# A bidirectional Mamba layer and a ConvLSTM on one core: dt and C copied to DRAM four times over before they are spread over the partitions

## The chip, the cores and the metric

The kernel runs on 1 core of a Trainium2 chip. The metric is the device time of one execution in microseconds (us). Before the change it is 7981.35 us, the median of 3 runs (7974.65 to 7982.71).

## The reference

The input is an image of 64 channels by 256 times by 128 frequencies, in float32. The first layer runs a bidirectional Mamba block along time and then another along frequency, each with a residual. The second layer is a windowed, bidirectional ConvLSTM. Everything that matters here is in the Mamba block:

```python
xdbl = jnp.einsum('nld,ed->nle', x, p['x_proj_w'])
dt, Bm, Cm = jnp.split(xdbl, [DT_RANK, DT_RANK + D_STATE], axis=-1)
dt = jax.nn.softplus(jnp.einsum('nlr,dr->nld', dt, p['dt_proj_w']) + p['dt_proj_b'])
A = -jnp.exp(p['A_log'])

def step(h, inp):
    dt_t, B_t, C_t, x_t = inp
    dA = jnp.exp(dt_t[:, :, None] * A)
    h = dA * h + dt_t[:, :, None] * B_t[:, None, :] * x_t[:, :, None]
    return (h, jnp.einsum('nds,ns->nd', h, C_t))
```

There are 128 inner channels (D_INNER) with 16 states each, so 2048 recurrences run side by side, forwards and backwards.

## The kernel before

**Tiles.** Stage 0 runs along time (sequences of 256 tokens), stage 1 along frequency (128 tokens). Each stage goes through 64 chunks of 512 tokens (NTOK), in two directions d. The 128 partitions of a scan hold 4 states (j, NJ) by 32 channels (DB); a row of a scan holds two states (g) by 512 tokens. A chunk and direction therefore has 8 scan steps: two groups of states (q) by 4 blocks of channels (b, NB). A chunk has 16 steps, and step S of the whole stage is step S mod 16 of its chunk.

**One step.** PE makes dt·B·x for the step (`inputs`, tile bx, L570) from dtxT and the diagonal matrices D (L460 on DVE). ACT makes exp(dt·A) (`decays`, tile dA, L590) from rep. DVE scans (`recur`, L598). POOL multiplies by C (`outputs`, L604). PE folds four steps into y (`add_up`, L613). DVE multiplies y by the gate (`gate`, tile yz, L629) at steps 2 and 10. A dA tile has four buffers, bx two, h seven.

**The spreads.** The decays need dt of 32 channels on 128 partitions, four times over, and POOL needs each of four rows of C on 32 partitions. Both go through DRAM. `dt_away` writes dt to the DRAM tile there in four transfers of 64 KB (L392); `project_bc` makes B and C with PE (L415), copies them out of PSUM with ACT (L424) and writes C to the DRAM tile away in four transfers of 8 KB per direction (L433). `spread_dt` (L475, tile rep, 3 buffers) and `spread_c` (L469, tile C, 3 buffers) read 512 KB each back, with the repetition in the source's access pattern. There are four of each per chunk. The source of `spread_c` has the shape 4 (j) by 32 (repeated) by 1024, that of `spread_dt` 4 (repeated) by 32 by 1024.

**Other transfers.** `normalise` (POOL, tile xn) writes the normalised input into the padded tile unp, by four transfers within SBUF (L308); `project_x` (L327, L328 on PE, copy L346 on ACT) and `project_z` read unp. In stage 0 `load` brings the input u (L282).

**Order.** Every engine works through its instructions in the order in which they are written, and all these transfers are issued by SyncE (SP). `Stage.run` goes through the steps S and writes, for each: the scan of S, outputs of S - 1, `add_up` when S mod 4 is 1, inputs and decays of S + 2, and then what the list HEAD has for that step. HEAD gives, for the chunk that begins at slot 16, the slot of each of its preparations: slot 6, for example, is step 6 of the chunk before, slot 17 is step 1 of its own, and half slots come after the closing of the chunk before. Negative slots lie one chunk earlier still. `first` prepares the first chunk of each stage, in an order of its own; SECOND is what it leaves to the loop.

The lines of HEAD that bear on the change are

```python
(-13, "load"),
(8, "project_bc", 0, 1),
(8, "dt_away", 0),
(8.5, "dt_away", 1),
(9.5, "spread_dt", 0, 0),
(10.5, "spread_c", 0, 0),
```

Of the kernel before, what the change touches and what calls it, by code (L numbers as in the profile page):

```python
# [29 lines left out]
F32 = mybir.dt.float32  # L30
# [6 lines left out]
P = 128  # L37
# [3 lines left out]
NS = 16  # L41
NBC = 2 * NS
NB = 4
NJ = 4
DB = P // NB
NU = 4
W = 64
RANK = 4
NTOK = 512
# [20 lines left out]


HEAD = (
    (-13, "load"),
    (-7.5, "squares"),
    (-6, "means"),
    (-6, "rms"),
# [4 lines left out]
    (6, "silus"),  # L81
    (6, "step_sizes"),
    (7, "softplus"),
    (8, "project_bc", 0, 1),
    (8, "dt_away", 0),
    (8.5, "dt_away", 1),
    (8.5, "times_x", 0),
    (9.5, "spread_dt", 0, 0),
    (10, "turn", 0),
    (10.5, "spread_c", 0, 0),  # L90
    (11, "diagonal", 0, 0, 0),
    (12, "spread_dt", 0, 1),
    (12.5, "times_x", 1),
    (13, "diagonal", 0, 0, 1),
    (13.5, "spread_c", 0, 1),
    (15, "diagonal", 0, 1, 0),
    (17, "diagonal", 0, 1, 1),
    (17, "spread_dt", 1, 0),
# [6 lines left out]
    (23, "diagonal", 1, 1, 0),  # L105
    (25, "diagonal", 1, 1, 1),
)
SECOND = tuple(x for x in HEAD if x[0] >= 12)


class Mamba:
# [3 lines left out]
    def __init__(self, ctx, tc, cols, room, d):  # L115
        nc = tc.nc
        self.nc, self.tc, self.d, self.cols = nc, tc, d, cols
        cp = ctx.enter_context(tc.tile_pool(name="m_const", bufs=1))
        self.ident = cp.tile([P, P], F32, name="ident")
        self.mask = cp.tile([P, W], F32, name="mask")  # L120
        self.fold = cp.tile([P, DB], F32, name="fold")
        self.ones = cp.tile([P, P], F32, name="ones")
        self.eps = cp.tile([P, 1], F32, name="eps")
        self.Wbc = cp.tile([P, 4, NBC], F32, name="wbc")
        self.cb, self.dtb, self.dp = (cols[:, 4 * n : 4 * n + 4] for n in range(3))
        self.A = cols[:, 12 : 12 + 4 * NS].rearrange("p (i n) -> p i n", i=4)
        self.G1, self.G2, self.Wz, self.Wdt, self.W2, self.W3 = ([] for _ in range(6))
        for i in range(4):
            for n, t, rows, width in (
                ("g1", self.G1, P, P),  # L130
                ("g2", self.G2, P, P),
                ("wdt", self.Wdt, P, P),
                ("w2", self.W2, P, C),
            ):
                t.append(cp.tile([rows, width], F32, name=f"{n}{i}", tag=f"{n}{i}"))
        for i in range(2):
            self.Wz.append(cp.tile([P, P], F32, name=f"wz{i}", tag=f"wz{i}"))
            self.W3.append(cp.tile([P, 2, C], F32, name=f"w3{i}", tag=f"w3{i}"))
        b = cp.tile([P, 2], F32, name="lin_b")
        self.b = b  # L140

        room = room.rearrange("p t f -> p (t f)")
        at = 0

        def take(rows, *shape):
            nonlocal at
            n = int(np.prod(shape))
            t = room[0:rows, at : at + n]
            at += n
            return t  # L150

        self.win = take(C, 4, 2 * P + 1).rearrange("p (i n) -> p i n", i=4)
        self.cw = take(C, 4, 4, P).rearrange("p (i k n) -> p i k n", i=4, k=4)
        self.xdt = take(RANK, 8, P).rearrange("p (i n) -> p i n", i=8)
        self.ow = take(C, 4, P).rearrange("p (i n) -> p i n", i=4)
        self.lin = take(C, 4, C).rearrange("p (i n) -> p i n", i=4)


        nc.vector.memset(self.ones, 0.0)
        for h in range(2):  # L160
            own = slice(h * C, (h + 1) * C)
            nc.vector.memset(self.ones[own, own], 1.0 / C)
        nc.vector.memset(self.eps, RMS_EPS)
        for w3 in self.W3:
            nc.vector.memset(w3, 0.0)
        make_identity(nc, self.ident)
# [57 lines left out]
class Stage:  # L224
# [162 lines left out]

    def dt_away(self, ch, d):

        there = self.dram.tile([DB, NB, NTOK], F32, name="there", tag="there")  # L390
        for b in range(NB):
            self.nc.sync.dma_start(out=there[:, b], in_=self.at["dt", ch, d][DB * b : DB * (b + 1)])  # L392
        self.at["there", ch, d] = there

    def in_turns(self, ap, order):

        return ap.rearrange(order, i=2, u=NU)

# [11 lines left out]
    def project_bc(self, ch, *ds):  # L410

        nc = self.nc
        pb = self.mm("pb")
        for d in ds:
            nc.tensor.matmul(  # L415
                pb[NBC * d : NBC * (d + 1)],
                lhsT=self.m.Wbc[:, 2 * self.stage + d],
                rhs=self.at["xs", ch, d],
                start=True,
                stop=True,  # L420
            )
        bc = self.wk.tile([2 * NBC, NTOK], F32, name="bc", tag="bc")
        rows = slice(NBC * ds[0], NBC * (ds[-1] + 1))
        nc.scalar.copy(  # L424
            self.in_turns(bc[rows], "p (u i c) -> p i u c"), self.in_turns(pb[rows], "p (i u c) -> p i u c")
        )
        for d in ds:
            away = self.dram.tile([NS // 2, 2, 2, NTOK // 2], F32, name="away", tag="away")
            for g in range(2):
                first = NBC * d + NS + NS // 2 * g  # L430
                c = self.in_turns(bc[first : first + NS // 2], "p (u i c) -> p i u c")
                for i in range(2):
                    nc.sync.dma_start(out=away[:, i, g].rearrange("a (u c) -> a u c", u=NU), in_=c[:, i])  # L433
            self.at["bc", d], self.at["away", ch, d] = bc[NBC * d : NBC * d + NS], away

    def turn(self, ch, d):
# [28 lines left out]

    def spread_c(self, ch, d, q):
        t = self.wk.tile([P, 2 * NTOK], F32, name="C", tag="C", bufs=3)
        away = self.at["away", ch, d].rearrange("(j q) i g t -> q j (i g t)", q=2)[q]
        self.nc.sync.dma_start(out=t, in_=away.unsqueeze(1).to_broadcast([NJ, DB, 2 * NTOK]))  # L469
        self.at["C", ch, d, q] = t  # L470

    def spread_dt(self, ch, d, h):
        t = self.wk.tile([P, 2, NTOK], F32, name="rep", tag="rep", bufs=NREP)
        there = self.at["there", ch, d]
        self.nc.sync.dma_start(  # L475
            out=t, in_=there[:, 2 * h : 2 * h + 2].unsqueeze(0).to_broadcast([NJ, DB, 2, NTOK])
        )
        self.at["rep", ch, d, h] = t

    def head(self, ch):  # L480
# [731 lines left out]
def _layouts(a):  # L1212

    L0 = {k[8:]: v for k, v in a.items() if k.startswith("L0_conv_")}
    L1 = {k[8:]: v for k, v in a.items() if k.startswith("L1_conv_")}

    def taps(w):

        return w.reshape(256, C, 4, 2, 5).transpose(3, 1, 4, 2, 0).reshape(P, 5, 4, 256)

    def gates(f, b):

        return np.concatenate([f.reshape(2, P), b.reshape(2, P)]).T

    return {
        "x": a["x"][0].transpose(0, 2, 1),
        "cols": np.concatenate(
            [
                L0["conv_b"].T,
                L0["dt_proj_b"].T,  # L1230
                L0["Dp"].T,

                L0["A_log"].reshape(4, NB, DB, NJ, 4).transpose(3, 2, 0, 1, 4).reshape(P, 4 * NS),
                gates(L1["b_ih_f"], L1["b_ih_b"]),
                gates(L1["b_hh_f"], L1["b_hh_b"]),
                np.tile(np.stack([L1["gln_g"], L1["gln_b"], L1["b_proj"]], 1), (2, 1)),
                np.broadcast_to(L1["prelu_a"].reshape(1, 1), (P, 1)),
            ],
            1,
        ),  # L1240

        "in_proj": np.concatenate([L0["in_proj_w"].transpose(2, 0, 1), L0["norm_w"].T[:, :, None]], 2),
        "conv_w": L0["conv_w"][:, :, 0, :].transpose(0, 2, 1),
        "dt_proj": np.concatenate(
            [L0["x_proj_w"][:, :RANK].transpose(1, 0, 2), L0["dt_proj_w"].transpose(2, 0, 1)], 1
        ),
        "x_proj_bc": np.concatenate(
            [L0["x_proj_w"][:, RANK : RANK + NS], L0["x_proj_w"][:, RANK + NS :: 2], L0["x_proj_w"][:, RANK + NS + 1 :: 2]], 1
        ).transpose(2, 0, 1),
        "out_proj": L0["out_proj_w"].transpose(1, 0, 2),  # L1250
        "lin_w": np.concatenate([L0[n + "_w"].reshape(2, C, C) for n in ("tlin", "flin")]).transpose(1, 0, 2),
        "lin_b": np.stack([L0["tlin_b"], L0["flin_b"]], 1),
        "W_ih_f": taps(L1["W_ih_f"]),
        "W_ih_b": taps(L1["W_ih_b"]),
        "W_hh_f": L1["W_hh_f"][:, :, 0].T,
        "W_hh_b": L1["W_hh_b"][:, :, 0].T,
        "W_proj": L1["W_proj"].reshape(P, C, 4, 2).transpose(0, 2, 3, 1).reshape(P, 4, P),
    }
# [18 lines left out]
```

## Time and profile before

| | |
|---|---|
| median of 3 runs | 7981.35 us |
| the profiled execution | 7979.07 us |
| its span | 7977.3 us |
| PE busy | 5895.4 us (74%) |
| DVE busy | 6357.9 us (80%) |
| ACT busy | 4741.7 us (59%) |
| POOL busy | 5563.0 us (70%) |
| DMA, hardware queue | 674.33 MB, 25.2% of 16 engines |
| mean granted TensorE clock | 0.895 |

Busy time is the time in which an engine carries out instructions, and the share is of the span. The last 690 us or so belong to the ConvLSTM, the rest to the two Mamba stages. Groups of instructions are named by their line; "x" counts them, and the number after the bar gives their busy time, the mean of one in ns, and the idle time of the engine just before them with what ended it. "SPq" is SyncE's queue, on which the row of a transfer is its issue, not its flight.

### The profile page before, as it was taken

How to read it: one execution, taken by the hardware profiler on the slowest of the kernel's cores; microseconds unless marked ns; L12 is line 12 of the kernel's file. 1: busy time of each engine (PE TensorE's matmuls, PEld its weight loads, DVE VectorE, ACT ScalarE, POOL GpSimd, SP SyncE). 2: the span in 40 equal slices, each digit the busy share in tenths (PEclk: the TensorE clock that was granted, in tenths of full speed). 3: DMA queues.
4: the chain of work that ended last, by engine and by line, in shares of the span. 5: the costliest groups of instructions: out<-in, count | busy, mean ns of one | idle time of the engine just before them, and what ended most of it. 6: DMA issues, size and time to landing. Idle time of an engine off the chain costs nothing. (4 is left out here: it accounts for less than half of the span.)

```text
span 7977.3 us, 325404 instructions
## 1 busy us (share of the span) xinstructions
PE 5895.4 (74%) x149512; PEld 3497.4 (44%) x149512; DVE 6357.9 (80%) x4166; ACT 4741.7 (59%) x8600; POOL 5563.0 (70%) x2898
## 2 busy tenths in 40 slices
PE   6776776767676776776777777777776777777999
PEld 3343433434343433333444444434443434335887
DVE  7887878788787878786788787878787878786887
ACT  6665666666565666665666565656565656664333
POOL 5776777677777777776777777777777767675554
PEclk8888988889898989888889888889898888888999
DMA  2222222222222222222222322222222222221000
GB/s 89 98 93 96 94 97 92 95 95 96 95 94 97 94 97 93 97 92 79 97 95 98 96 95 94 92 91 92 93 91 94 92 93 91 94 89 72 13 15 17
DMA packets 302064, 695.14 MB, mean 87 GB/s; under 512 B 72852, under 2 KB 129812, under 8 KB 300696
## 3 DMA queue, kind: packets, MB, share of 16 engines
q1 hardware_dynamic: 300696, 674.33, 25.2%
q8 instruction: 1173, 19.22, 1.1%
q14 instruction: 195, 1.60, 0.1%
HBM read 557.25 MB, written 83.89 MB: 80 GB/s over the span
## 5 line engine op out<-in xcount | busy, mean ns | idle before, releaser
L604 POOL TENSOR_TENSOR h<-h,C 128x1024 f32<-128x1024 f32 x2048 | 4821.6, 2372 | 1782.9 <-DVE h L598 1282.2
L598 DVE TENSOR_TENSOR_SCAN h<-dA,bx 128x1024 f32<-128x1024 f32 x2048 | 4615.6, 2276 | 1403.8 <-ACT dA L590 1063.9
L590 ACT ACTIVATE dA<-rep,cols 128x510 f32<-128x510 f32 (+1 forms) x4096 | 2648.1, 711 | 874.6 <-DMA rep<-there 874.6
L570 PE MATMUL bx<-D,dtxT 64*32 64x128 f32 x131072 | 2418.5, 281 | 900.3 <-DVE h L598 880.8
L570 PEld LDWEIGHTS bx<-D,dtxT 64*32 64x32 f32 x131072 | 1901.4, 108 | 2044.1 <-issue 881.7
L460 DVE TENSOR_TENSOR D<-mask,bt 128x1024 f32<-128x1024 f32 x1026 | 1226.7, 1196 | 10.8 <-PE bt L447 10.8
L613 PE MATMUL y<-h,fold 128*32 128x512 f32 x8192 | 1212.2, 660 | 5.0 <-POOL h L604 5.0
L327 PE MATMUL px<-unp,g 128*128 128x512 f32 x504 | 399.8, 886 | 1067.3 <-DMA unp<-xn 1067.3
L346 ACT ACTIVATE xs<-px,cols 128x512 f32<-128x512 f32 x252 | 173.4, 688 | 1191.6 <-PE px L328 1191.5
L327 PEld LDWEIGHTS px<-unp,g 128*128 128x128 f32 x504 | 100.3, 249 | 1123.3 <-DMA unp<-xn 903.9
L613 PEld LDWEIGHTS y<-h,fold 128*32 128x32 f32 x8192 | 257.6, 116 | 596.9 <-issue 585.5
L403 POOL TENSOR_TENSOR dtx<-dt,xs 128x512 f32<-128x512 f32 x256 | 327.7, 1280 | 80.4 <-ACT dt L379 80.4
L328 PE MATMUL px<-unp,g 128*128 128x512 f32 x504 | 365.9, 819 | 0.0
L449 ACT COPY dtxT<-pt 128x512 f32<-128x512 f32 x256 | 149.8, 585 | 312.4 <-PE pt L445 312.3
L369 PE MATMUL pv<-xs,wdt 128*128 128x512 f32 x512 | 276.9, 666 | 49.0 <-ACT xs L363 47.5
L328 PEld LDWEIGHTS px<-unp,g 128*128 128x128 f32 x504 | 132.6, 263 | 190.5 <-issue 190.5
L1162 POOL TENSOR_TENSOR y<-v,X 128x512 f32<-128x512 f32 x32 | 40.6, 1269 | 231.2 <-DVE v L1160 231.2
L587 ACT COPY dA<-zeros 128x4 f32<-128x4 f32 (+1 forms) x1024 | 197.5, 193 | 2.2 <-DVE h L598 0.8
L629 DVE TENSOR_TENSOR yz<-y,zs 128x512 f32<-128x512 f32 x256 | 171.4, 670 | 13.5 <-PE y L613 10.8
L625 ACT ACTIVATE y<-xs,cols 128x512 f32<-128x512 f32 x256 | 175.6, 686 | 7.0 <-DVE yz L629 7.0
L671 PE MATMUL po<-yz,w 128*64 128x256 f32 x1024 | 170.9, 399 | 0.0
L445 PE MATMUL pt<-ident,dtx 128*128 128x128 f32 x1024 | 168.6, 287 | 0.8 <-POOL dtx L403 0.8
(189 smaller groups left out, 5122.5 us busy)
## 6 DMA issues: line engine op xcount, KB each, us to landing
rep<-there SPq DMA_DIRECT2D x512, 512.0 KB
C<-away SPq DMA_DIRECT2D x512, 512.0 KB
there<-dt SPq DMA_DIRECT2D x1024, 64.0 KB
unp<-xn SPq DMA_DIRECT2D x504, 64.0 KB
away<-bc SPq DMA_DIRECT2D x1024, 8.0 KB
u<-in_x SPq DMA_DIRECT2D x128, 64.0 KB
out<-y SPq DMA_DIRECT2D x32, 256.0 KB
w<-in_W_ih_f SPq DMA_DIRECT2D x10, 512.0 KB
```

The lines of the kernel that those rows point to most:

```text
L327: nc.tensor.matmul(self.seqs(px), lhsT=m.G1[i], rhs=self.unp[:, :, first : first + L], start=True, stop=False)
L328: nc.tensor.matmul(self.seqs(px), lhsT=m.G2[i], rhs=self.unp[:, :, second : second + L], start=False, stop=True)
L369: self.nc.tensor.matmul(pv, lhsT=self.m.Wdt[i], rhs=self.at["xs", ch, d], start=True, stop=True)
L403: self.nc.gpsimd.tensor_mul(self.in_turns(dtx, own), self.in_turns(self.at["dt", ch, d], natural), self.in_turns(self.at["xs", ch, d], nat ...
L460: self.nc.vector.tensor_mul(D, self.m.mask.unsqueeze(1).unsqueeze(1).to_broadcast([P, n, 2, W]), b.unsqueeze(3).to_broadcast([P, n, 2, W]),)
L570: self.nc.tensor.matmul(bx[DB * j : DB * (j + 1), i, :, u], lhsT=dtxT[rows, u, DB * b : DB * (b + 1)], rhs=D[rows, u, j], start=True, stop ...
L587: nc.scalar.copy(dA[:, :, :, :, first : first + 1], self.zeros)
L590: nc.scalar.activation(dA[:, :, g, :, live], rep[:, :, :, live], AF.Exp, scale=m.A[:, k, n : n + 1])
L598: self.nc.vector.tensor_tensor_scan(h[:, step], dA[:, step], bx[:, step], 0.0, ALU.mult, ALU.add)
L604: self.nc.gpsimd.tensor_mul(h, h, self.at["C", ch, d, q])
L613: nc.tensor.matmul(y[DB * b : DB * (b + 1)].rearrange("p (i t) -> p i t", i=2), lhsT=self.m.fold, rhs=hs[b][:, g], start=False, stop=q == ...
L625: self.nc.scalar.mul(self.y, self.at["xs", ch, d], self.m.dp[:, i : i + 1])
```

## The change

`dt_away` writes each block of dt four times, once for each j, so that there has four copies; `spread_dt` then reads 128 rows, each once. `project_bc` makes C twice in PSUM: the rows for B in the order of before (they are copied to bc with the tokens in turns, and the C rows beside them there are padding), and C's 16 rows, in another order, in the upper 64 partitions, which a second ACT copy takes over in token order. away has four copies of each row of C (NR), and `spread_c` reads 16 rows (4 states by 4 copies), each repeated 8 times. The weights for this projection double in size, to 128 KB, with zero padding. In HEAD `dt_away` of direction 0 comes ahead of `project_bc`, `dt_away` of direction 1 moves from slot 8.5 to slot 14, the first `spread_c` from 10.5 to 10, and `load` from -13 to -12.

```diff
+NR = 4
...
-    (-13, "load"),
+    (-12, "load"),
...
+    (8, "dt_away", 0),
     (8, "project_bc", 0, 1),
-    (8, "dt_away", 0),
-    (8.5, "dt_away", 1),
...
-    (10.5, "spread_c", 0, 0),
+    (10, "spread_c", 0, 0),
...
+    (14, "dt_away", 1),
...
-SECOND = tuple(x for x in HEAD if x[0] >= 12)
+SECOND = tuple(x for x in HEAD if x[0] >= 12 and x[1] != "dt_away")
...
-        there = self.dram.tile([DB, NB, NTOK], F32, name="there", tag="there")
+        there = self.dram.tile([NJ, DB, NB, NTOK], F32, name="there", tag="there")
         for b in range(NB):
-            self.nc.sync.dma_start(out=there[:, b], in_=self.at["dt", ch, d][DB * b : DB * (b + 1)])
+            dt = self.at["dt", ch, d][DB * b : DB * (b + 1)]
+            self.nc.sync.dma_start(
+                out=there[:, :, b].rearrange("j d t -> d j t"), in_=dt.unsqueeze(1).to_broadcast([DB, NJ, NTOK])
+            )
...
+        for n in range(2):
+            for d in ds:
+                first = 2 * NBC * n + NBC * d
+                nc.tensor.matmul(
+                    pb[first : first + NBC],
+                    lhsT=self.m.Wbc[:, 2 * self.stage + d, n],
...
+        rows = slice(2 * NBC + first, 2 * NBC + last)
+        nc.scalar.copy(bc[rows], pb[rows])
         for d in ds:
-            away = self.dram.tile([NS // 2, 2, 2, NTOK // 2], F32, name="away", tag="away")
+            away = self.dram.tile([NS // 2, NR, 2, 2, NTOK // 2], F32, name="away", tag="away")
             for g in range(2):
-                first = NBC * d + NS + NS // 2 * g
-                c = self.in_turns(bc[first : first + NS // 2], "p (u i c) -> p i u c")
+                first = 2 * NBC + NBC * d + NS // 2 * g
+                c = bc[first : first + NS // 2].rearrange("p (i t) -> p i t", i=2)
                 for i in range(2):
-                    nc.sync.dma_start(out=away[:, i, g].rearrange("a (u c) -> a u c", u=NU), in_=c[:, i])
+                    nc.sync.dma_start(
+                        out=away[:, :, i, g], in_=c[:, i].unsqueeze(1).to_broadcast([NS // 2, NR, NTOK // 2])
+                    )
...
-        away = self.at["away", ch, d].rearrange("(j q) i g t -> q j (i g t)", q=2)[q]
-        self.nc.sync.dma_start(out=t, in_=away.unsqueeze(1).to_broadcast([NJ, DB, 2 * NTOK]))
+        away = self.at["away", ch, d][NJ * q : NJ * (q + 1)].rearrange("j r i g t -> (j r) (i g t)")
+        self.nc.sync.dma_start(out=t, in_=away.unsqueeze(1).to_broadcast([NJ * NR, DB // NR, 2 * NTOK]))
...
-        there = self.at["there", ch, d]
-        self.nc.sync.dma_start(
-            out=t, in_=there[:, 2 * h : 2 * h + 2].unsqueeze(0).to_broadcast([NJ, DB, 2, NTOK])
-        )
+        there = self.at["there", ch, d].rearrange("j d b t -> (j d) b t")
+        self.nc.sync.dma_start(out=t, in_=there[:, 2 * h : 2 * h + 2])
```

More of the change, by code (lines that the diff above doesn't have):

```diff
@@ L123, in __init__ @@
         self.eps = cp.tile([P, 1], F32, name="eps")
-        self.Wbc = cp.tile([P, 4, NBC], F32, name="wbc")
+        self.Wbc = cp.tile([P, 4, 2, NBC], F32, name="wbc")
         self.cb, self.dtb, self.dp = (cols[:, 4 * n : 4 * n + 4] for n in range(3))
@@ L413, in project_bc @@
         pb = self.mm("pb")
[L414 to L420, printed above, removed]
-            )
-        bc = self.wk.tile([2 * NBC, NTOK], F32, name="bc", tag="bc")
-        rows = slice(NBC * ds[0], NBC * (ds[-1] + 1))
+        for n in range(2):
[4 more added lines that the diff above has]
+                    lhsT=self.m.Wbc[:, 2 * self.stage + d, n],
+                    rhs=self.at["xs", ch, d],
+                    start=True,
+                    stop=True,
+                )
+        bc = self.wk.tile([P, NTOK], F32, name="bc", tag="bc")
+        first, last = NBC * ds[0], NBC * (ds[-1] + 1)
+        rows = slice(first, last)
         nc.scalar.copy(
@@ L426, in project_bc @@
         )
+        rows = slice(2 * NBC + first, 2 * NBC + last)
+        nc.scalar.copy(bc[rows], pb[rows])
         for d in ds:
-            away = self.dram.tile([NS // 2, 2, 2, NTOK // 2], F32, name="away", tag="away")
+            away = self.dram.tile([NS // 2, NR, 2, 2, NTOK // 2], F32, name="away", tag="away")
             for g in range(2):
-                first = NBC * d + NS + NS // 2 * g
-                c = self.in_turns(bc[first : first + NS // 2], "p (u i c) -> p i u c")
+                first = 2 * NBC + NBC * d + NS // 2 * g
+                c = bc[first : first + NS // 2].rearrange("p (i t) -> p i t", i=2)
                 for i in range(2):
-                    nc.sync.dma_start(out=away[:, i, g].rearrange("a (u c) -> a u c", u=NU), in_=c[:, i])
+                    nc.sync.dma_start(
+                        out=away[:, :, i, g], in_=c[:, i].unsqueeze(1).to_broadcast([NS // 2, NR, NTOK // 2])
+                    )
             self.at["bc", d], self.at["away", ch, d] = bc[NBC * d : NBC * d + NS], away
@@ L473, in spread_dt @@
         t = self.wk.tile([P, 2, NTOK], F32, name="rep", tag="rep", bufs=NREP)
-        there = self.at["there", ch, d]
-        self.nc.sync.dma_start(
-            out=t, in_=there[:, 2 * h : 2 * h + 2].unsqueeze(0).to_broadcast([NJ, DB, 2, NTOK])
-        )
+        there = self.at["there", ch, d].rearrange("j d b t -> (j d) b t")
+        self.nc.sync.dma_start(out=t, in_=there[:, 2 * h : 2 * h + 2])
         self.at["rep", ch, d, h] = t
@@ L1246, in _layouts @@
         ),
-        "x_proj_bc": np.concatenate(
-            [L0["x_proj_w"][:, RANK : RANK + NS], L0["x_proj_w"][:, RANK + NS :: 2], L0["x_proj_w"][:, RANK + NS + 1 :: 2]], 1
-        ).transpose(2, 0, 1),
+        "x_proj_bc": np.pad(
+            np.stack(
+                [
+                    L0["x_proj_w"][:, RANK : RANK + NS],
+                    L0["x_proj_w"][:, RANK + NS :].reshape(4, NJ, 2, 2, P).transpose(0, 3, 2, 1, 4).reshape(4, NS, P),
+                ],
+                1,
+            ),
+            ((0, 0), (0, 0), (0, NBC - NS), (0, 0)),
+        ).transpose(3, 0, 1, 2),
         "out_proj": L0["out_proj_w"].transpose(1, 0, 2),
```

## The prediction

> **What bounds the kernel now.** I read the page first: busy shares, the DMA row, the costliest groups. No engine is full: DVE, the busiest, has 80%. The DMA row stands at 2 tenths (once 3) for thirty-six of forty slices.
>
> ```profile
> DMA  2222222222222222222222322222222222221000
> ...
> L598 DVE TENSOR_TENSOR_SCAN h<-dA,bx 128x1024 f32<-128x1024 f32 x2048 | 4615.6, 2276 | 1403.8 <-ACT dA L590 1063.9
> L590 ACT ACTIVATE dA<-rep,cols 128x510 f32<-128x510 f32 (+1 forms) x4096 | 2648.1, 711 | 874.6 <-DMA rep<-there 874.6
> ...
> L327 PE MATMUL px<-unp,g 128*128 128x512 f32 x504 | 399.8, 886 | 1067.3 <-DMA unp<-xn 1067.3
> ```
>
> Followed back, the scan waits for ACT's decays, and these wait for the dt spread (rep), or stand behind a copy of px that waits for PE, which waits for unp, a transfer inside SBUF. Then I read the timeline of one chunk. The columns are start, duration, engine, line; the bracket holds the idle time before and what ended it.
>
> ```profile
> 2049.46 2.70 SPq L433 DMA_DIRECT2D away<-bc  x8
> 2052.21 5.20 SPq L392 DMA_DIRECT2D there<-dt  x8
> 2057.51 0.53 SPq L475 DMA_DIRECT2D rep<-there  x1
> 2058.09 0.51 SPq L469 DMA_DIRECT2D C<-away  x1
> 2058.70 2.53 SPq L308 DMA_DIRECT2D unp<-xn  x4
> ...
> 2066.75 1.33 ACT L590 ACTIVATE dA<-rep,cols 128x510 f32<-128x510 f32 x2 [7.03 <-DMA rep<-there]
> ...
> 2078.75 2.29 DVE L598 TENSOR_TENSOR_SCAN h<-dA,bx 128x1024 f32<-128x1024 f32 x1 [8.30 <-ACT dA L590]
> ```
>
> The spread of dt, issued at 2057.5, lands at 2066.75. In the same view PE starts px at 2072.88, released by unp, 11.65 us after unp's last issue ended (2061.23). In the first chunk, where no spread is under way, unp's issues end at 48.81 and px starts at 50.40: 1.6 us. So 10 us are queueing. What is queued shows in the stretches (columns: stretch, length, PE, PEld, DVE, ACT, POOL busy, TensorE clock, DMA share, GB/s):
>
> ```profile
> 2012.00:2016.00 4.00, 0.00 (x0) 0.00 (x0) 1.50 (x1) 0.00 (x0) 0.43 (x2) 0.52 0.26 96
> ...
> 2036.00:2040.00 4.00, 3.39 (x112) 1.49 (x95) 4.00 (x3) 4.00 (x9) 4.00 (x2) 1.00 0.30 86
> ```
>
> With only spreads in flight the DMA share is 0.25 and the rate about 105 GB/s: 4 of 16 engines. The spreads' access patterns have 4 rows outermost (NJ). The weight loads of the last layer have 128 rows outermost, and between 7292 and 7300 they show
>
> ```profile
> DMA  0087436899579998999999999999999999999999
> ```
>
> with most slices from 390 to 450 GB/s; I take 420. Both give 26 GB/s per engine. The bound now is the queue on four engines in the stretch from dt to the next chunk's second step; everywhere else DVE is full (4.00 of 4.00 in 2036:2040).
>
> **DVE's own pace.** In that unstalled stretch:
>
> ```profile
> 2032.88 4.46 DVE L598 TENSOR_TENSOR_SCAN h<-dA,bx 128x1024 f32<-128x1024 f32 x2
> 2037.25 1.20 DVE L460 TENSOR_TENSOR D<-mask,bt 128x1024 f32<-128x1024 f32 x1
> 2038.36 4.46 DVE L598 TENSOR_TENSOR_SCAN h<-dA,bx 128x1024 f32<-128x1024 f32 x2
> ```
>
> Two steps with one D take 5.48 to 5.49 us. A chunk has 16 steps, 8 D and 2 gates; a gate (yz, 2051.53 to 2052.12) adds 0.58. So 8 x 5.49 + 2 x 0.58 = 45.1 us. Now a chunk takes 56.1 (scan at 2022.64 to scan at 2078.75).
>
> The scans of stage 0 run from 46.82 to 3631.92, those of stage 1 from 3665.65 to 7284.94: 3585.1 + 3619.3 = 7204.4 us for 128 chunks, 56.02 and 56.55 each. The profiled execution took 7979.07 (span 7977.3), 2 us under the median of 7981.35. Outside the scans lie 7979.07 - 7204.4 = 774.7 us, which I leave as they are. At DVE's pace the scans take 128 x 45.1 = 5773, so the floor is 6547.7.
>
> **The change, part by part,** on the clock of the chunk above, whose step 8 starts at 2043.85.
>
> *Bytes.* Per chunk now: spreads 8 x 512 KB, there 512, unp 256, u 128, away 64. A low engine carries 1024 + 56 + 8 KB = 1.11 MB, 42 us at 26.3 GB/s of the 56. After: the spreads' 4096 KB over 16 engines, there 2048, away 256 on 8 engines, unp and u as before: at most 440 KB per engine, 17 us. Each spread drops from about 5 us (128 KB per engine) to 1.25 us (32 KB).
>
> *dt_away ahead of C's copy, half of it later.* dt of the first direction is ready at 2045.6. Its four writes, now 256 KB each, issue first: 4 x 0.65 us at the dearest row, done by 2048.2. Now they stand behind away, which waits for bc until 2049.4 (SP's wait at L433 is 1655 us in all). The 1 MB needs 2.5 us at 420 GB/s. No row shows DRAM writes at full load: at the 105 GB/s of four engines it would be 10 us, and the check below holds even so, just. I take 420, because these writes have 32 rows outermost.
>
> *C's copy in token order.* Two more pairs of matmuls on PE (L415: 138.3 us for 128 chunks, so 1.08 more) and one more ACT copy (L424, 0.56). The copy is done at 2050.0, the eight away issues (2.70 in all) at 2052.8.
>
> *First spreads.* rep issues at 2053.3 and lands 1.25 + 1.6 later, 2056.2; the decays of step 16 start at step 14, 2060.9: 4.7 us of cover. C waits for away to land, until 2054.4 at the latest row (1.6), and is issued at 2055. Behind this wait on SP stand the four unp transfers, whose data (xn) is ready only at 2056.15: nothing lost. unp's issues end at 2058.7; it lands at 2060.3, or 2062.8 if both spreads are still ahead of it. At DVE's pace PE reaches px after step 14's scan and the bx of step 16, 2060.91 + 2.29 + 1.16 = 2064.4. So unp is early by 1.6 to 4 us where it is 8.5 us late now, and the 8.30 us idle of the fence goes.
>
> *dt_away of the second direction at step 14.* Four issues, 2.6 us, behind the second rep and C, ahead of the spread at step 17 (2068.6), which needs them landed: 2063.5 + 2.5 + 1.6 = 2067.6. That spread's first decays are at step 22: 10 us of cover. The u load one step later moves SP's wait for po (989.9 us in all) past nothing that is due.
>
> *What is late next.* POOL has 16 x 2.37 + 2 x 1.28 + 0.72 = 41.2 us per chunk, ACT 36, both under 45.1; PE about 42 (5895.4 less 650.4 of the last layer, over 128, plus 1.08), part of it at the lower clock. So DVE, with these remainders per chunk:
> - the gate at step 2, where PE has px, the sums into y and bx in a row: idle of 0.15 + 0.45 us in the timeline before 2028.42 and 2029.56: 0.6.
> - the decays of step 17 stand behind px: bx 1.16, px 2.0, copy 0.7, decays 1.4 end 7.8 us after step 14 starts, and step 17 is due at 7.7: 0.1.
> - the same at the lower clock: px's four matmuls take 2.05 + 1.91 at clock 0.5 (2072.88) against 1.13 + 1.02 at 1.0, 1.8 more. Of two chunks read, one had a lowered clock at step 13 (0.62, and a wait of 0.56 for bx before step 14). Bounds 0 and 2.4; I take a third, 0.8.
> - PE's extra 1.08 us just fits before step 11: 0.1. DMA bursts beside DVE: the copy L883 takes 3.24 us beside the weight loads and 3.17 alone, 2% in a third of the time: 0.2.
>
> That is 1.8; stage 1, 0.5 dearer per chunk now, gets 0.2 more: 1.9 x 128 = 243, and 6547.7 + 243 = 6790.
>
> On the clock the stretches show 0.50 to 0.62 after idle gaps of PE and 1.00 elsewhere. The Trainium skill, TensorE: Matmul & The Clock Gate, Part 1, says that an idle window of about 3.4 us halves the clock and a busy one restores it. By that rule, once the 8 us gap is gone no gap here is long enough, the third remainder is nil, and the sum would be 6547.7 + 128 x 1.1 = 6690. I keep 0.8, because the lowering at 2003 followed gaps of only 2.2 us.
>
> **The rivals.**
>
> *PE takes DVE's place.* PE would have 42 of 45 us, and works in written order; if it runs at the lower clock from step 13 to 17 in every chunk, px twice, pz and three bx (2 x 2.0 + 1.13 + 3 x 1.16) take about twice as long and some 5 us more come into each chunk: 6547.7 + 128 x 6.8 = 7420. For it: half clock in one chunk of two at step 13. Against: after the stalls px is back at full clock within 5 us. 0.15, with times from 7080 to 7500.
>
> *The spreads stay on four engines*, because C's source repeats each of its 16 rows eight times and no row of this trace shows that pattern; the same for rep would need the merged (j d) rows to be taken apart again. Then the fourfold writes only add: there 96 KB and away 24 KB more per low engine and chunk, 4.7 us at 26.3 GB/s, in the stretch that already ends last: 7979 + 128 x 4.7 = 8580, slower. It decides only if both spreads fail: with one spread moved, a low engine has some 30 us of work in 47. Against it: there<-dt, with 32 rows, lifts the share to 0.6, and 128 rows to 0.9. 0.05. The Trainium skill, DMA: Bandwidth & Descriptors, on why a DMA increments its semaphore by 16, makes the number of engines the largest up to 16 that divides the slowest dimension of both sides; by it this rival falls away, and the 0.25 agrees with it.
>
> *The gain goes elsewhere*, to a wait of equal length that I don't see, within 0.2% of now: 0.01.
>
> **How the numbers follow.** Forecast 0.79: DVE bound, 6790. Its own range is 6610 (remainders 0.5) to 7080 (remainders 4.2: lower clock in every chunk, 2.4 for 0.8, and unp late by 0.7 behind slow writes). That holds 8 in 10, so it is the range. 0.2%, 16 us, is about what a measurement of this kernel can tell. Faster 0.94, same 0.01, slower 0.05.
>
> **What would show it.** Right: DMA slices peaking at 6 to 9 tenths with gaps between; DVE idle for dA from 1064 to under 150 us; unp's wait at L327 gone from 1067; DVE above 90% through the first layers; rep landing within 4 us of its issue; PE's clock near 1.0. Wrong: a DMA share still at 0.25 between bursts (rival two); scans waiting for PE bx L570 by several us per chunk (rival one); L590 still waiting for rep, which would mean that the DRAM writes are slow.

## The result, and the profile after

The changed kernel takes 7165.55 us (median of 4 runs, 7155.95 to 7175.18) against 7981.19 us (median of 4): a ratio of 0.898, 95% interval 0.896 to 0.900. It is 10% faster, where 15% was forecast, and lies 86 us above the upper end of the range. The profiled execution took 7169.17 us (span 7167.4).

The page after, with the groups that answer to those of before (the scan is now L607, bx L579, the decays L599):

```profile
DMA  5555555555555555545555555555555555550000
...
L607 DVE TENSOR_TENSOR_SCAN h<-dA,bx 128x1024 f32<-128x1024 f32 x2048 | 4618.0, 2276 | 497.4 <-PE bx L579 310.4
L579 PE MATMUL bx<-D,dtxT 64*32 64x128 f32 x131072 | 2509.0, 281 | 1180.5 <-DVE h L607 799.5
...
L599 ACT ACTIVATE dA<-rep,cols 128x510 f32<-128x510 f32 (+1 forms) x4096 | 2648.1, 710 | 171.2 <-DMA rep<-there 163.7
...
L328 PE MATMUL px<-unp,g 128*128 128x512 f32 x504 | 313.7, 706 | 46.5 <-DMA unp<-xn 46.3
```

The waits that bounded the kernel are nearly gone: px waited 1067 us for unp and waits 46, the decays waited 875 us for rep and wait 164, and DVE's idle time before the scan fell from 1404 to 497 us. But the first cause of that idle time is a new one. DVE waits for bx, 310 us against 117 before. The list of waits says what PE does in that time (engine, line, what ended the wait, us in total, times, longest):

```profile
PE bx L579 <- issue: 371.7, 266, 4.7
DVE h L607 <- PE bx L579: 310.4, 261, 4.5
DVE h L607 <- ACT dA L599: 157.8, 96, 10.1
```

"issue" is a wait with no semaphore behind it: PE had nothing to wait for, and no instruction. Before, the rows of these two waits were

```profile
DVE h L598 <- PE bx L570: 116.8, 146, 3.2
PE bx L570 <- issue: 11.9, 18, 1.5
```

In PE's timeline the holes lie inside a group of 64 matmuls, which nothing but PE's own stream can interrupt:

```profile
2060.59 0.44 PE L579 MATMUL bx<-D,dtxT 64*32 64x128 f32 x15
2061.93 0.94 PE L579 MATMUL bx<-D,dtxT 64*32 64x128 f32 x49 [0.90 <-issue]
...
2094.07 1.03 PE L579 MATMUL bx<-D,dtxT 64*32 64x128 f32 x50 [1.39 <-issue]
```

The instructions come by DMA, on queue q8. The page counts 1173 packets there before and 1177 after, 16 KB each, and PE has 1024 instructions more after (512 matmuls and 512 weight loads of the second projection): 256 per packet. The DMA queues (packets, MB, share of 16 engines) from 2055 to 2059, and from 2059 to 2062, where the first hole lies:

```profile
q1 hardware_dynamic: 190, 0.57, 49.5%
```

```profile
q1 hardware_dynamic: 237, 0.55, 72.7%
q8 instruction: 1, 0.02, 2.1%
```

In the first 4 us, in which a spread of dt and then one of C begin, no instruction packet starts; one starts in the next 3. In the records the packet before starts at 2052.51, this one at 2059.53; it ends at 2060.54, and 1.39 us later PE goes on. Of the 251 holes of over 0.3 us inside a group of bx (367 us together), the middle eight tenths end 1.26 to 1.58 us after a packet of q8 ended. And when the instructions of PE's records are counted from the start of the program, all 251 holes end at the same place of a block of 256: PE has then issued 193 or 194 instructions of its block. So PE starves for instructions, as the seam of two packets would have it, when a fetch comes late. What DMA is doing at such times shows in the stretches (columns as before):

```profile
2084.00:2086.00 2.00, 0.69 (x50) 0.42 (x39) 2.00 (x2) 1.21 (x2) 2.00 (x2) 1.00 1.09 260
2086.00:2088.00 2.00, 1.00 (x64) 0.70 (x44) 2.00 (x2) 0.00 (x0) 2.00 (x2) 1.00 1.05 278
```

A share of 1 is all 16 engines at work. Before, the spreads kept four busy and left twelve.

### The profile page after: what moved, and what is told of

Read it like the earlier page. It is cut to its first block, busy times and chain, and to the rows that moved or that the text cites. A ratio compares the mean times of both kernels' runs of the same rounds, so it can differ in the third digit from the quotient of the medians.

```text
span 7167.4 us, 327118 instructions
## 1 busy us (share of the span) xinstructions
PE 5830.0 (81%) x150024; PEld 3482.0 (49%) x150024; DVE 6368.4 (89%) x4166; ACT 4829.9 (67%) x8730; POOL 5567.1 (78%) x2898
## 3 DMA queue, kind: packets, MB, share of 16 engines
q8 instruction: 1177, 19.28, 1.1%
## 4 chain that ended last, share of the span: by engine, by line
PE 25%; DVE 11%; ACT 8%; issue 6%; DMA 2%; POOL 2%; SPq 1%; DVEq 0%; POOLq 0%; ACTq 0%
DVE h L607 8%; PE bx L579 6%; PE cv L1048 6%; ACT dA L599 4%; PE y L622 3%; DVE D L471 2%; PE px L328 2%; PE px L329 1%; POOL h L613 1%; PE pv L370 1%; DMA unp<-xn 1%; PE pz L334 1%; PE pg L1104 1%; PE both L1160 1%; ACT L387 1%
## 5 line engine op out<-in xcount | busy, mean ns | idle before, releaser
L607 DVE TENSOR_TENSOR_SCAN h<-dA,bx 128x1024 f32<-128x1024 f32 x2048 | 4618.0, 2276 | 497.4 <-PE bx L579 310.4
L579 PE MATMUL bx<-D,dtxT 64*32 64x128 f32 x131072 | 2509.0, 281 | 1180.5 <-DVE h L607 799.5
L579 PEld LDWEIGHTS bx<-D,dtxT 64*32 64x32 f32 x131072 | 1926.4, 108 | 2312.4 <-issue 1125.7
L599 ACT ACTIVATE dA<-rep,cols 128x510 f32<-128x510 f32 (+1 forms) x4096 | 2648.1, 710 | 171.2 <-DMA rep<-there 163.7
L622 PE MATMUL y<-h,fold 128*32 128x512 f32 x8192 | 1106.4, 659 | 5.4 <-POOL h L613 5.4
L328 PE MATMUL px<-unp,g 128*128 128x512 f32 x504 | 313.7, 706 | 46.5 <-DMA unp<-xn 46.3
L329 PE MATMUL px<-unp,g 128*128 128x512 f32 x504 | 277.3, 633 | 0.5 <-issue 0.5
L355 ACT COPY zs<-pz 128x512 f32<-128x512 f32 x252 | 134.9, 586 | 154.5 <-PE pz L334 148.6
L1120 ACT ACTIVATE a<-pg,cols,scale 128x488 f32<-128x488 f32 x128 | 86.5, 756 | 135.6 <-DVE pg L1118 135.6
L380 ACT ACTIVATE dt<-pv,cols 128x512 f32<-128x512 f32 x256 | 164.3, 684 | 12.7 <-issue 6.2
```

The costliest lines, as they stand in the source:

```text
L328: nc.tensor.matmul(self.seqs(px), lhsT=m.G1[i], rhs=self.unp[:, :, first : first + L], start=True, stop=False)
L329: nc.tensor.matmul(self.seqs(px), lhsT=m.G2[i], rhs=self.unp[:, :, second : second + L], start=False, stop=True)
L579: self.nc.tensor.matmul(bx[DB * j : DB * (j + 1), i, :, u], lhsT=dtxT[rows, u, DB * b : DB * (b + 1)], rhs=D[rows, u, j], start=True, stop ...
L599: nc.scalar.activation(dA[:, :, g, :, live], rep[:, :, :, live], AF.Exp, scale=m.A[:, k, n : n + 1])
L607: self.nc.vector.tensor_tensor_scan(h[:, step], dA[:, step], bx[:, step], 0.0, ALU.mult, ALU.add)
L622: nc.tensor.matmul(y[DB * b : DB * (b + 1)].rearrange("p (i t) -> p i t", i=2), lhsT=self.m.fold, rhs=hs[b][:, g], start=False, stop=q == ...
```

## The experiments

Three theories for the 376 us between 6790 and 7166: F, late instruction fetches; W, the fourfold writes, which land late; K, PE's lowered clock. Ratios are to the kernel before, run beside it on the same chip; the changed kernel's is 0.898. "PE bx <- issue" is the row above.

**e1, e2: more traffic that nobody waits for.**

```diff
+    (18.5, "idle_copy", 0),
...
+    (19.5, "idle_copy", 1),
...
+    (22.5, "idle_copy", 2),
...
+    (23.5, "idle_copy", 3),
...
+        to = self.dram.tile([16, 8, 1024], F32, name="idle", tag="idle", bufs=4)
+        self.nc.sync.dma_start(out=to[:, 0:7], in_=...)
```

In e2 the tile is [4, 29, 1024], of which 28 rows are used.

> The changed kernel and four extra copies per chunk at steps 2, 3, 6 and 7, of 448 KB each from the input to a DRAM tile that nobody reads, with 16 rows outermost. Theory F (PE gets its instructions late: they are fetched by DMA in blocks of 16 KB, 1177 on queue q8, and a fetch has to queue when all 16 engines are in a burst): PE bx <- issue rises from 372 us to over 550, and the time by 1 to 4%, 7240 to 7450, though no data waits for these copies. Theory W (the rest of the gap is the fourfold writes, which land late): within 0.5% of 7166, since nothing due soon is queued behind the copies. Theory K (PE's lowered clock at steps 13 to 15): no change.

> The same extra bytes at the same steps, but with 4 rows outermost, so on 4 engines. Theory F: twelve engines stay free for the fetches, PE bx <- issue stays at 372 or below 420, the time within 0.7% of the changed kernel's, well below the copies on 16 engines. Theory W: the same as with 16 rows or worse, since each low engine gets four times as much (4.3 us per copy). Theory K: no change.

e1: 7313.42 us, 0.918 (0.916 to 0.920). e2: 7141.10 us, 0.896 (0.895 to 0.898). Their rows:

```profile
PE bx L590 <- issue: 497.0, 343, 4.3
```

```profile
PE bx L590 <- issue: 363.6, 260, 3.7
```

Theory F was right in sign and place. 16 engines raise PE's wait by 125 us (I expected over 178) and the time by 2%; the same bytes on 4 engines change neither. W and K expected no difference between them.

In the records up to 17 packets of the idle copies are in flight at once in e1 and mostly three to five in e2, as 16 and 4 engines would have it.

**e3: 16 engines in another way.** One copy of dt and of C, and four transfers per spread, each of 32 rows:

```diff
+        for j in range(NJ):
+            self.nc.sync.dma_start(out=t[DB * j : DB * (j + 1)], in_=there)
...
+        for j in range(NJ):
+            self.nc.sync.dma_start(out=t[DB * j : DB * (j + 1)], in_=away[NJ * q + j].to_broadcast([DB, 2 * NTOK]))
```

> No fourfold writes: there and away have one copy, and each spread is four transfers, one for each j, with 32 rows outermost, so still 16 engines. Bytes per chunk fall from 6784 to about 5000 KB, and SP issues 24 transfers more per chunk (some 13 us). Theory W: what was missing goes, 6790 to 6900. Theory F: the bursts of reads are as before and only those of the writes go: PE bx <- issue falls from 372 to between 150 and 300, time 6950 to 7100. Theory K: 7166, or more if unp comes later behind the additional issues.

6684.14 us, 0.838 (0.837 to 0.840).

```profile
L608 DVE TENSOR_TENSOR_SCAN h<-dA,bx 128x1024 f32<-128x1024 f32 x2048 | 4602.3, 2274 | 135.2 <-PE bx L580 78.8
```

```profile
PE bx L580 <- issue: 10.9, 26, 1.0
```

Faster than any theory said. DVE idles 135 us before its scans, and PE waits 10.9 us for instructions, as little as before the change, though the spreads bring the same 4 MB per chunk on 16 engines. F as I had put it (any burst of reads) is too wide. W seemed right, but e3 changes two things: the writes and the form of the spreads. The scans take 46.2 us per chunk here, 1.1 above DVE's own pace.

**e4: direction 1 as before, on four engines, with C in token order.**

```diff
+        n = NJ if d == 0 else 1
+        there = self.dram.tile([n, DB, NB, NTOK], F32, name="there", tag=f"there{d}")
...
+        if d == 0:
+            there = self.at["there", ch, d].rearrange("j d b t -> (j d) b t")[:, 2 * h : 2 * h + 2]
+        else:
+            there = self.at["there", ch, d][:, :, 2 * h : 2 * h + 2].to_broadcast([NJ, DB, 2, NTOK])
```

The copies of C and their spreads likewise.

> Direction 0 as in the changed kernel; direction 1 with one copy of dt and C and spreads with 4 rows outermost, as before. 21 us per chunk on four engines, which are free from step 17 to step 8 of the next chunk. Theory F: only the bursts between steps 8 and 14 are left on 16 engines, PE bx <- issue falls below 200, time 6850 to 7020. Theory W: half of the writes go, 6950 to 7050, with PE bx <- issue unchanged. Theory K: 7166; if the spreads of direction 1 then land too late for steps 8 and 10, ACT dA <- DMA rep rises above 164 us and the time above 7166.

6801.79 us, 0.854 (0.852 to 0.855), PE bx <- issue 154.4 us. Half of the whole spreads are gone, and so is over half of the wait; the time is below all that was expected. W's row (unchanged wait) is out.

**e5, e6: is it writes or reads?** Theory F now comes in versions: what holds up a fetch is writes to DRAM (F-write), any bytes on 16 engines (F-bytes), or transfers that bring 32 KB or more to each engine (F-size); for e9 to e14 also the rows of the whole spread's pattern (F-rows). On top of e3, six transfers per chunk of 256 KB at steps 2 to 8, from SBUF to DRAM (e5) or from DRAM to SBUF (e6), 128 rows of 2 KB:

```diff
+        to = self.dram.tile([P, 512], F32, name="idle_to", tag="idle_to", bufs=4)
+        self.nc.sync.dma_start(out=to, in_=self.idle)
```

```diff
+        t = self.wk.tile([P, 512], F32, name="idle", tag="idle", bufs=1)
+        self.nc.sync.dma_start(out=t, in_=src[:, 512 * (k % 2) : 512 * (k % 2 + 1)])
```

> The split kernel (one copy, spreads in four transfers; PE bx <- issue 10.9 us) and six writes of 256 KB per chunk from a tile that stays as it is to a DRAM tile nobody reads, 128 rows of 2 KB, 16 engines, at steps 2 to 8. Theory F-write (a fetch is held up by writes to DRAM on its engine): PE bx <- issue rises above 150 us, time above 6800. Theory F-size (it is held up by transfers with 32 KB or more per engine, as the whole spreads and the 448 KB copies are): these have 16 KB each, so it rises a little, below 80, time 6700 to 6760. Theory F-bytes (any byte on 16 engines): as the reads of the next kernel.

> The split kernel and six reads of 256 KB per chunk at the same steps, from the input in DRAM to an SBUF tile that nobody uses, 128 rows of 2 KB, 16 engines. F-write: PE bx <- issue stays below 40 us, time 6690 to 6740 (SP issues six more). F-bytes: the same rise as with the writes. F-size: below 80.

e5: 6709.60 us, 0.842 (0.840 to 0.844), wait 34.3 us. e6: 6703.74 us, 0.842 (0.839 to 0.844), wait 40.4 us. No difference between writes and reads, and little of either, in the range of F-size. F-write is out.

**e7: the fourfold writes with spreads in four transfers.**

```diff
+        for j in range(NJ):
+            self.nc.sync.dma_start(out=t[DB * j : DB * (j + 1)], in_=there[j, :, 2 * h : 2 * h + 2])
```

C's spreads likewise, from one of the four copies.

> The changed kernel's fourfold writes, but each spread in four transfers with 32 rows outermost, each from one copy. F-write: PE bx <- issue stays above 250 us and the time at 7050 to 7200. F-size: it falls below 120, time 6750 to 6900. F-bytes: as the changed kernel, 7166, since the bytes are the same.

6823.46 us, 0.856 (0.854 to 0.859), wait 29.8 us:

```profile
PE bx L583 <- issue: 29.8, 64, 1.7
```

With as many bytes as the changed kernel, on as many engines and in packets of the same 4 KB, all but 30 us of the wait for instructions are gone, and 342 us of time. So it is the form of the spread: one transfer with 32 KB for each engine, or four with 8 KB. What is left of theory W is the 139 us by which e7 is slower than e3: unp lands late again here (px waits 139.6 us for it, against 8.3 in e3). SP's lists ahead of it are longer: eight issues of away with four copies take 5.76 us (2054.95 to 2060.71), with one copy 2.64 in e3.

**e9: halves.** The changed kernel, each spread as two transfers by columns, C's likewise:

```diff
-        self.nc.sync.dma_start(out=t, in_=there[:, 2 * h : 2 * h + 2])
+        for b in range(2):
+            self.nc.sync.dma_start(out=t[:, b], in_=there[:, 2 * h + b])
```

> The changed kernel, but each spread is two transfers, each of one half of the columns: the same rows outermost, the same engines, the same bytes, 16 KB instead of 32 KB per engine and transfer, rows of 2 KB instead of 4 KB. F-size (a fetch is held up behind one transfer's share of an engine): PE bx <- issue falls from 372 us to below 120, time 6800 to 6950. F-rows (it is the spread's pattern, 16 or 128 rows with one engine reading its own rows): 372 stays, time 7150 to 7250.

6784.52 us, 0.853 (0.851 to 0.855).

```profile
PE bx L584 <- issue: 119.2, 128, 3.0
```

At 16 KB per engine and transfer the wait is 119 us, between 372 at 32 KB (the changed kernel) and 30 at 8 KB (e7). Five per cent come back by cutting each spread in two. The halves also have packets of 2 KB; e7's quarters do not.

**e10, e11, e13, e14: which spread?** e10 has dt's part of the change alone, e11 C's part alone, the other on four engines; in e13 and e14 the other has one copy and spreads in four transfers, as in e3. e10 against the changed kernel, and e11, each with the writes that belong to it:

```diff
-        self.nc.sync.dma_start(out=t, in_=away.unsqueeze(1).to_broadcast([NJ * NR, DB // NR, 2 * NTOK]))
+        self.nc.sync.dma_start(out=t, in_=away.unsqueeze(1).to_broadcast([NJ, DB, 2 * NTOK]))
```

```diff
-        self.nc.sync.dma_start(out=t, in_=there[:, 2 * h : 2 * h + 2])
+        self.nc.sync.dma_start(
+            out=t, in_=there[:, 2 * h : 2 * h + 2].unsqueeze(0).to_broadcast([NJ, DB, 2, NTOK])
+        )
```

> The part for dt alone: fourfold writes of dt and spreads of dt from 128 rows; C copied once, in turns, and spread on four engines. The new order is kept. F-size: half of the whole spreads are left on 16 engines, PE bx <- issue between 120 and 250; C on four engines takes 21 us per chunk and ends in time; 6950 to 7100. F-rows with C at fault: issue below 60. With dt at fault: issue near 372.

> The part for C alone: four copies of C, spread from 16 rows; dt written once and spread on four engines. F-size: PE bx <- issue between 120 and 250, as with dt alone; without the 2 MB of dt's writes 6850 to 7100, more if the first spread of dt, 5 us on four engines, is late for step 16. F-rows with C at fault: issue near 372; with dt at fault: below 60.

> C as in the changed kernel (four copies, one transfer of 32 KB per engine from 16 rows), dt with one copy and spreads in four transfers. F-size: PE bx <- issue between 60 and 200 us, about the same as in e14; 6720 to 6850. F-rows with C at fault: above 150 here and below 40 in e14.

> dt as in the changed kernel (fourfold writes, one transfer of 32 KB per engine from 128 rows), C with one copy and spreads in four transfers. F-size: PE bx <- issue between 60 and 200 us, about the same as in e13; with the fourfold writes 6800 to 6950. F-rows with C at fault: below 40, and the time near 6820, that of the fourfold writes with split reads.

e10: 6949.75 us, 0.872 (0.870 to 0.875), wait 57.2. e11: 7680.70 us, 0.966 (0.964 to 0.967), wait 177.0; its decays wait 1015.9 us for rep, which is on four engines again, and the time is far above what I expected. e10's 57.2 is less than half of what F-size said, and where C's rows as the cause would put it; but e11's 177.0 is not near the 372 that goes with them. In these two the queue on four engines differs as well, so they do not decide. e13: 6818.97 us, 0.856 (0.854 to 0.857); e14: 6738.48 us, 0.846 (0.844 to 0.847). Their rows, e13 first:

```profile
PE bx L577 <- issue: 65.3, 93, 2.7
```

```profile
PE bx L582 <- issue: 72.7, 102, 2.5
```

Alike, as F-size said, so it is not the pattern of C's rows. Each kind of whole spread alone costs some 70 us of PE's wait, both together 372: more than the sum. And e14, with the fourfold writes of dt, is only 54 us slower than e3, including its PE wait, and below the 6800 to 6950 that I expected: the 2 MB of writes per chunk cost little. e13 has C's four copies, and px waits 105.1 us for unp.

**e8, e12, e15: the order and the 16 engines.** e8 is the kernel before with the new list alone. e12 is e3 with C's part of before (one ACT copy, C in turns). e15 is the kernel before with nothing but spreads in four transfers:

```diff
+        for j in range(NJ):
+            self.nc.sync.dma_start(
+                out=t[DB * j : DB * (j + 1)], in_=away[2 * j + q : 2 * j + q + 1].to_broadcast([DB, 2 * NTOK])
+            )
...
+        for j in range(NJ):
+            self.nc.sync.dma_start(out=t[DB * j : DB * (j + 1)], in_=there)
```

> The kernel before with the new order of SP's transfers alone: one copy, spreads on four engines, C's copy in turns. All theories: a low engine still has 42 us of spreads in a chunk, and unp still queues behind them; the first spread is issued about 4 us earlier, so 2 to 5 us per chunk are won, 7350 to 7750; PE bx <- issue stays near 12 us.

> The kernel before with nothing changed but the spreads, each in four transfers with 32 rows outermost: one copy of dt and C, C in turns, the old order. If the queue on four engines was the bound, most of the gain comes from this alone: 6700 to 6900, a little above e12 (6677), since the first spread is issued some 4 us later and has 4.7 us of cover. If the order mattered most: above 7200.

> The split kernel with the C part of before: one ACT copy, one pair of matmuls per direction, C in turns. 1.08 us of PE and 0.56 us of ACT per chunk go, both beside DVE: 6640 to 6690, against 6684. If the away writes of 256 B rows are slower, C waits longer and unp behind it: up to 6720.

e8: 7605.24 us, 0.955 (0.952 to 0.957). e15: 6960.93 us, 0.874 (0.872 to 0.876), above what I expected. e12, which has both: 6677.16 us, 0.839 (0.838 to 0.841). The order alone brings 4.5%, the 16 engines alone 12.6%, both 16.1%. In e15 px waits 258.1 us for unp, and 281 of the 297 us that DVE waits for dA there, followed back in the records, lie behind a px that waited so. In the old order all eight transfers of dt are issued ahead of unp; in the new one four are. e12 and e3 are the fastest, as good as equal: C's copy in token order brings nothing that can be measured once no copies are needed.

## Why the prediction was wrong, point by point

**Right.** The bound: four engines with the spreads of the whole chunk, seen at a share of 0.25. e15, where 16 engines alone bring 12.6%, and e11, where dt's spreads on four engines bring the wait for rep back, show it from both sides. Followed back in the records, 1039 of the 1064 us that DVE waited for dA before lie behind a px that waited for unp, so that was the branch that cost. DVE's pace of 45.1 us per chunk: in e3 every instruction of DVE from 2039.66 to 2089.96 follows the one before without a gap that matters, as in

```profile
2045.74 4.46 DVE L608 TENSOR_TENSOR_SCAN h<-dA,bx 128x1024 f32<-128x1024 f32 x2
2050.12 1.20 DVE L468 TENSOR_TENSOR D<-mask,bt 128x1024 f32<-128x1024 f32 x1
2051.23 4.46 DVE L608 TENSOR_TENSOR_SCAN h<-dA,bx 128x1024 f32<-128x1024 f32 x2
```

with 5.49 us for two steps. What lies outside the scans, 774.7 us, was 773.3. unp's wait went but for 46 us. The rival of spreads that stay on four engines fell, and with it the slower side.

**The step that failed** is "What is late next". Its list of remainders said 1.9 us per chunk. The scans of the changed kernel run from 45.46 to 3211.34 and from 3243.51 to 6473.46, 49.97 us per chunk: 4.87 above DVE's pace. The missing 3.0 us, times 128, are the 380 us between 6790 and the profiled 7169. PE's wait for instructions grew by 360 us, 2.8 per chunk. The list named DVE, POOL, ACT and PE, and not PE's instruction stream, though the page of before had it: 19.22 MB on q8, beside the queue whose spreads the change was about to put on all 16 engines. The sum counted the twelve free engines as room; that a fetch there has to share them is what e1 shows against e2. DVE meets it in its waits for bx (310 us, 117 before) and for y at the gates (73, 11 before), and behind px in those for dA:

```profile
2038.81 2.07 PE L328 MATMUL px<-unp,g 128*128 128x512 f32 x2
...
2042.29 0.69 ACT L347 ACTIVATE xs<-px,cols 128x512 f32<-128x512 f32 x1 [7.15 <-PE px L329]
...
2044.38 2.29 DVE L607 TENSOR_TENSOR_SCAN h<-dA,bx 128x1024 f32<-128x1024 f32 x1 [3.08 <-ACT dA L599]
```

Just ahead of this px a group of bx had a hole of 1.90 us, up to 2037.80. Of the 158 us that DVE waits for dA, 73 lie behind a px that had such a hole in the 10 us ahead of its copy, and 43 behind one that waited for unp alone. e3 shows the rest of the list by itself: 1.1 us per chunk above DVE's pace, with 10.9 us of waits for instructions.

**A mis-sized term.** 420 GB/s for the fourfold writes. The first two microseconds with nothing but dt's writes in full flight show

```profile
2070.00:2072.00 2.00, 2.00 (x24) 0.52 (x16) 2.00 (x3) 1.96 (x6) 2.00 (x2) 1.00 0.95 200
```

200 GB/s at a share of 0.95. From the first scan to the last the hardware queue's packets take 26.9 us of 16 engines per chunk, where I had 17: a packet of 4 KB takes 244 ns on average, against 176 before and the 156 that 26.3 GB/s would give. The eight away issues, put at 2.7 us, take 5.75 (2072.54 to 2078.29), and the first spread lands 5.5 us after its issue (2078.34 to 2083.88) instead of 2.9. The cover of 4.7 us held for rep: ACT waits 164 us for it, but of DVE's waits for dA only 2 us follow from that directly. For unp, which SP issues behind away, the cover failed in part (the 43 us above); in e7 130 us of DVE's waits for dA lie behind a px that waited for unp.

**The clock.** At 0.946 it rose, but the matmuls at L328 still average 706 ns and those at L329 633, where 589 is the shortest; in e3, at 0.967, they average 648 and 596. In e10 they are as slow as in the changed kernel (694 and 661) and the time is 216 us less, and e9, at 0.967, is 381 us faster. So theory K falls as the cause of most of the loss. The holes can lower the clock in their turn: from 2034 to 2038 PE is busy for 0.83 of 4 us, and from 2038 to 2040 the granted clock is 0.59. The third remainder was therefore not nil here. What this costs in all was not separated.

The rival in which PE takes DVE's place named the right engine: 4.87 us per chunk lie between the forecast's 1.9 and its 6.8, the measured 7166 us lies within its 7080 to 7500, and its sign, scans waiting for bx, came with 2.4 us per chunk. But that is luck: it priced the lower clock, and what came were late instructions; PE is busy 81%.

**What stays open.** That a whole spread holds up a fetch and four quarters do not is shown by e7, e9, e13 and e14. The records also show that the fetch starts late rather than runs long. Its packet takes 1.09 us (median) in the changed kernel, 1.12 before and 1.15 in e3; but from the moment that PE passes a fixed place of its block of 256 to the start of the next packet go 2.6 us (median), where it was 1.2 before and 1.3 in e3, and ahead of the holes 5.2. Why it starts late is not shown: either a fetch stands behind what one transfer has queued on its engine, or four transfers, each issued half a microsecond after the other, leave gaps. In e3 the share over 2 us moves between 0.14 and 1.05 while spreads are issued; in the changed kernel it stays at 0.92 or more from 2080 to 2090. No run tells size from pace. Nor does any show why two kinds of whole spread cost more than the sum of each.

## What to carry to other kernels

When a transfer is spread over all DMA engines, look at who else uses DMA: PE reads the instructions of this program, 150 thousand matmuls and as many weight loads, in 1177 packets of 256, and "issue" holes inside a group of matmuls are the sign that they come late. Copies that nobody waited for cost 2% on 16 engines (e1) and nothing on four (e2). And outermost rows were to be had here by cutting a transfer (four by 32 rows) rather than by copying the data: e15 has 12.6% with two edited functions.

## What was not expected of the hardware

PE ran out of instructions for 372 us in all, with single holes up to 4.7 us, in a kernel with 81% of PE busy. The Trainium skill, Runtime: NRT & Kernel Launch, Instruction fetch mechanics, has the engines fetch blocks of 16 KB over their own DMA queue while the current one runs, and calls this hidden. The size agrees with the trace; that it is hidden holds before (11.9 us) and in e3 (10.9), not in the changed kernel.

The fourfold writes of dt to DRAM, from 32 rows each, ran at 200 GB/s on a share of 0.95, where the weight loads of before ran at about 420. Writing to DRAM is not slow as such: where no other transfer was issued near them, a packet of 2 KB took 150 ns on average in dt's writes here, 131 in e3, where they are single, and 88 in e5's writes from 128 rows. So the 32 rows go with most of the slowness and the four copies with some; which of their properties does it was not tried.
